# Self-attention in a decoder-and-fusion kernel: which key slot is reused first, and which score blocks come first

## The chip, the cores and the metric

One core of one Trainium2 chip runs the whole program. The metric is device time in microseconds (us); the median of three runs is given. TensorE is called PE in the views, VectorE DVE, ScalarE ACT, GpSimd POOL, and SyncE SP; SP issues most of the DMAs, in the order of its queue.

## The reference

The input is x, 4 batches of 1024 tokens of 512 channels, and a short context. A decoder layer comes first (self-attention, cross-attention, feed-forward, each with a layer norm and a residual), then a fusion with a gate. Only self-attention is touched by the change. It has 16 heads of 32 channels and is causal:

```python
q = einsum('btc,hcd->bhtd', xn, Wq) + bq      # k and v likewise
scores = einsum('bhtd,bhsd->bhts', q, k) / scale
scores = where(tril, scores, -inf)
attn = softmax(scores, axis=-1)
out = einsum('bhts,bhsd->bhtd', attn, v)
```

## The kernel before

**Units.** Self-attention is done in 32 units. A unit is a batch b (4), a group g of four heads (4), and a half h of the queries (2). With few exceptions h = 0 holds query tiles 0, 1, 6, 7 of 128 tokens and h = 1 holds tiles 2, 3, 4, 5, so that both have the same amount of causal work; in the first group of the first batch they are 0 to 3 and 4 to 7. The keys of a group stand in two halves, m = 0 (tokens 0 to 511) and m = 1 (512 to 1023). Both units of a group use the same two halves, except the very first unit, which needs m = 0 alone.

**Stacks.** Queries and keys are projected, split in a high and a low part, and stored to DRAM (L623, tensors `qd` and `kd`). `load_stacks` (L648) brings them back as stacks in SBUF: four key slots (`ks0` to `ks3`), one per key half, and three query slots (`qs0` to `qs2`), one per unit. `pile` (L641) loads one stack with three DMAs of 256 KB on SP's queue (L646). A list `order` keeps the key slots by age: a half that is not there yet goes into the oldest slot that none of the units in work needs, and each slot that a unit uses goes to the young end, in the order in which the loop (L652) meets the halves. The stacks of unit u + 2 are asked for when unit u begins.

**Two passes over the scores.** The first pass, `maxima` (L672), computes scores of a unit with queries on the rows, one PSUM bank of 512 columns at a time (L692, tiles `s`, four banks, shared with the projections), and VectorE takes the row minimum of each block (the scores are negated): with `tensor_reduce` (L702) where no mask is needed, with a masked custom operation (L699) and a read of its result on the diagonal. `put_maxima` (L716) combines them, transposes them on PE (`tpm`, L726), splits them in two rows (`mT`, L728 and L729) and sends them by ScalarE's DMA queue into two more rows of the query stack (L732). The second pass, `attend` (L735), computes the scores again with keys on the rows and with the maxima already subtracted (L755, tiles `st`, 98 rows instead of 96), takes the exponential on ScalarE (L760), masks the diagonal on POOL (L768), multiplies by the values (L785, `av`) and adds up the denominators, mostly on POOL (L809). For h = 1 it goes through the key tiles in the order 0, 5, 1, 4, 2, 3, so that the half m = 1 is done with before m = 0 is.

**A unit's score blocks.** There are 18 banks in a unit. A bank is a full block of 512 columns, or a pair of smaller ones: 128 and 384 columns of one head, or 256 and 256 of two heads. `maxima` writes them out head by head (L707 to L713): first the pair 128 and 384, then from every second head the pair 256 and 256, then the full blocks.

**What sets the order.** `run` (L115) merges three streams by the columns of work that they have done: the `attend` steps of unit u, the score steps still open of unit u + 1 with the first eight steps of unit u + 2 (L947 to L952; the first step only makes tiles, so seven banks), and projections of later groups (L854 to L871). Each engine then works in a fixed order, which the program's scheduler settles at build time from its own estimates, with priorities by stream.

Of the kernel before, what the change touches and what calls it, by code (L numbers as in the profile page):

```python
# [18 lines left out]
P = 128  # L19
# [10 lines left out]
HG = P // DH  # L30
# [22 lines left out]
def decoder_then_fusion(ctx: ExitStack, tc: tile.TileContext, x, ctxT, cols, rows,  # L53
# [399 lines left out]
    def self_attention(ph):  # L453
# [183 lines left out]
        def keys_of(u):  # L637
            b, g, _, tiles = units[u]
            return [(b, g, m) for m in range(tiles[-1] // NJ + 1)]

        def pile(stack, src, parts):  # L641

            for i, k in enumerate(parts):
                nc.sync.dma_start(raw(stack)[i * DH : (i + 1) * DH], src[k].rearrange("(r d) t -> d r t", d=DH))  # L646

        def load_stacks(u, since):  # L648

            b, g, h, _ = units[u]  # L650
            used = {k for w in range(since, u + 1) for k in keys_of(w)}
            for m, key in enumerate(keys_of(u)):  # L652
                if key in k_held:
                    slot = k_held.index(key)
                else:
                    slot = next(i for i in order if k_held[i] not in used)
                    k_held[slot] = key
                    pile(k_stacks[slot], k_dram[b, m, g], (0, 0, 1))
                order.remove(slot)
                order.append(slot)  # L660
                k_at[u, m] = k_stacks[slot]
            if (b, g) not in v_at:
                v_at[b, g] = vp.tile([P, NT, P], F32, tag="v", name=f"v_{b}_{g}")
            new = [key[2] for key in keys_of(u) if key not in v_held]
            v_held.update(keys_of(u))
            if new:
                kbs = slice(new[0] * NJ, (new[-1] + 1) * NJ)
                nc.sync.dma_start(v_at[b, g][:, kbs], v_dram[b,][:, kbs, g * P : (g + 1) * P])
            q_at[u] = q_stacks[u % len(q_stacks)]
            pile(q_at[u], q_dram[b, h, g], (0, 1, 0))  # L670

        def maxima(u):  # L672

            tiles = units[u][3]
            held = {}

            def begin():

                held["top"] = small.tile([P, HG, NJ, NG], F32, tag="top", name=f"top_{u}", bufs=2)
                held["least"] = small.tile([P, HG, NJ], F32, tag="least", name=f"least_{u}", bufs=2)  # L680

            def width(tile, m):
                return min(TG, (tile + 1) * P - m * TG)

            def scores(blocks):

                sc = ps_s.tile([P, TG], F32, tag="s", name="s_%d_%d_%d_%d" % (u, *blocks[0]))
                parts, at = [], 0
                for r, j, m in blocks:
                    part = sc[:, at : at + width(tiles[j], m)]  # L690
                    at += width(tiles[j], m)
                    nc.tensor.matmul(part, q_at[u][:KS, r, j * P : (j + 1) * P],  # L692
                                     k_at[u, m][:KS, r, : part.shape[-1]], start=True, stop=True)
                    parts.append(part)
                for part, (r, j, m) in zip(parts, blocks):
                    far = tiles[j] >= NJ
                    dst = held["top"][:, r, j, m : m + 1] if far else held["least"][:, r, j : j + 1]
                    if m == tiles[j] // NJ:
                        nc.vector.tensor_tensor_reduce(part, part, mask[:, TG - part.shape[-1] :],  # L699
                                                       1.0, TOP, ALU.add, ALU.min, dst)  # L700
                    else:
                        nc.vector.tensor_reduce(dst, part, AX.X, ALU.min)  # L702

            steps = [(0, begin)]
            at_width = {width(t, t // NJ): (j, t // NJ) for j, t in enumerate(tiles)}
            full = [(j, m) for j, t in enumerate(tiles) for m in range(t // NJ + 1) if width(t, m) == TG]
            for r in range(HG):  # L707

                banks = [[(r, *at_width[P]), (r, *at_width[3 * P])]] + [[(r, *at)] for at in full]
                if r % 2:  # L710
                    banks.insert(1, [(r - 1, *at_width[2 * P]), (r, *at_width[2 * P])])
                steps += [(sum(width(tiles[j], m) for _, j, m in blocks), lambda blocks=blocks: scores(blocks))
                          for blocks in banks]  # L713
            return steps + [(0, lambda: put_maxima(u, held["top"], held["least"]))]

        def put_maxima(u, top, least):  # L716

            tiles, qs = units[u][3], q_at[u]  # L720
            far = [j for j, tile in enumerate(tiles) if tile >= NJ]
            if far:
                nc.vector.tensor_reduce(least[:, :, far[0] :], top[:, :, far[0] :], AX.X, ALU.min)
            rows = HG * NJ
            tp = ps_of[Z["tpm"]][0].tile([rows, P], F32, tag=ps_of[Z["tpm"]][1], name=f"tpm_{u}")
            nc.tensor.transpose(tp, least.rearrange("p r j -> p (r j)"), ident)  # L726
            mT = [small.tile([rows, P], FR, tag=f"mT{k}", name=f"mT{k}_{u}", bufs=1) for k in range(2)]
            nc.vector.tensor_scalar(mT[0], tp, -1.0, None, ALU.mult)  # L728
            nc.vector.scalar_tensor_tensor(mT[1], tp, -1.0, mT[0], ALU.mult, ALU.subtract)  # L729

            for k in range(2):
                nc.scalar.dma_start(raw(qs[KS + k : KS + k + 1].rearrange("p r (j q) -> p (r j) q", q=P)),  # L732
                                    raw(mT[k]))
# [139 lines left out]
        def loads(u, since):  # L873
            return [(0, lambda: load_stacks(u, since))]

        run(pieces[0])
        early_banks[:] = Z["eb1"]
        load_stacks(0, 0)
        run(maxima(0), pieces[1] + loads(1, 0), speed=(Z["sp0"], 1))
        k = int(len(pieces[AHEAD]) * Z["p4f"])  # L880
        pieces[AHEAD + 1] = pieces[AHEAD][k:] + pieces[AHEAD + 1]
# [57 lines left out]
        for u in range(len(units)):  # L939
            if u and u + 2 < len(units):  # L940
                load_stacks(u + 2, u)
            main, tail = attend(u, tail)
            n = u % 2
            ahead, begun = begun, []
            if not ahead and u + 1 < len(units):
                ahead = maxima(u + 1)
            if u and u + 2 < len(units) and Z["phi%d" % n]:  # L947
                begun = maxima(u + 2)
                k = Z["phi%d" % n]
                first = begun[: k]  # L950
                first.insert(Z["tpl"], ahead.pop())
                ahead, begun = ahead + first, begun[k:]  # L952
            if u == first_late:
                fronts_of.close()
                rest = late_steps()
                total = sum(t for t, _ in rest)
            if u >= first_late:
                fill, part = [], Z["late"][u - first_late] * total
                while rest and (part > 0 or u + 1 == len(units)):
                    part -= rest[0][0]  # L960
                    fill.append(rest.pop(0))
            else:
                fill = pieces[u + AHEAD]
            run(main, ahead, fill, speed=(Z["main"], (Z["ahead%d" % n] if u < Z["alf"] else Z["ahead_l"]) if u else Z["a0"], Z["fill"]), sooner=(Z["so0"], Z["so1"], Z["so2"]))
# [842 lines left out]
```

## Time and profile before

| | us |
|---|---|
| median of 3 runs | 2146.06 |
| lowest, highest | 2144.63, 2152.42 |
| the profiled execution's own time | 2153.24 |
| its span, first to last instruction | 2151.5 |
| PE busy (of the span) | 2064.3 (96%) |
| DVE busy | 1452.1 (67%) |
| POOL busy | 1210.7 (56%) |
| ACT busy | 967.5 (45%) |

The profiled execution is 7.2 us over the median of the timed runs and near their highest. Self-attention takes the first 930 us or so: the last `st` product starts at 930.3 us. Engines' busy times overlap; the one that is busy nearly throughout is the one to look at first. Idle time of an engine is listed with what ended it, and of the other engines it costs nothing in itself. The granted clock of PE is given with the windows; 1.00 is full speed.

### The profile page before, as it was taken

To read this page: it belongs to the slowest core of one execution; us is meant where nothing else is said; L and a number is where in the kernel's file an instruction comes from. 1 tells how busy PE (TensorE), PEld (TensorE's weight loads), DVE (VectorE), ACT (ScalarE), POOL (GpSimd) and SP (SyncE) were. 2 spreads that over 40 slices of the span, in tenths; PEclk is the share of its full clock that TensorE was granted. 3 is DMA by queue.
4 is the path that set the end of the run, shared out by engine and by line. 5 is a ranking of instruction groups with operands and counts; after the bars stand their busy time and mean duration, and the time that the engine had idled before them with its cause. 6 is when DMAs were issued, how large, how long until landed. Compare 5 with 4: busy or idle time off the path is not lost.

```text
span 2151.5 us, 34750 instructions
## 1 busy us (share of the span) xinstructions
PE 2064.3 (96%) x11544; PEld 1568.7 (73%) x11544; DVE 1452.1 (67%) x3134; ACT 967.5 (45%) x2180; POOL 1210.7 (56%) x1257
## 2 busy tenths in 40 slices
PE   6999998999999989989999999999999999999997
PEld 5766676667667756457888887788788888888885
DVE  6587757665755587567676776877667846865667
ACT  3365555555565545435555557433322422232222
POOL 3288878888788877774555543512343524433323
PEclk9999999999999998999999999999999999999998
DMA  8866767677666567662323122965576457655631
GB/s 245 258 186 168 218 203 216 182 243 219 190 174 186 158 171 213 206 204 79 99 84 103 50 79 86 332 210 170 182 238 198 166 175 237 207 175 171 220 113 39
DMA packets 241321, 379.36 MB, mean 176 GB/s; under 512 B 35948, under 2 KB 104284, under 8 KB 239094
## 3 DMA queue, kind: packets, MB, share of 16 engines
q1 hardware_dynamic: 215532, 348.32, 52.4%
q10 hardware_dynamic: 25610, 28.83, 4.4%
q8 instruction: 92, 1.51, 0.3%
q14 instruction: 87, 0.71, 0.1%
HBM read 251.71 MB, written 124.81 MB: 175 GB/s over the span
## 4 chain that ended last, share of the span: by engine, by line
PE 76%; DMA 7%; DVE 7%; POOL 4%; issue 2%; ACT 1%; SPq 1%; ACTq 0%; DVEq 0%; POOLq 0%
PE acc L1495 15%; PE ph L1473 14%; PE st L755 5%; PE s L692 5%; PE av L785 5%; PE po_c L102 4%; PE pq_x L102 3%; PE pk L102 3%; PE pv L102 3%; PE pg_o L102 3%; PE po_x L102 3%; PE pq L102 3%; POOL pT L809 2%; PE sc_c L87 2%; PE av_c L1139 1%
## 5 line engine op out<-in xcount | busy, mean ns | idle before, releaser
L809 POOL TENSOR_TENSOR pT<-pT,pT 128x256 f32<-128x256 f32 (+3 forms) x369 | 551.6, 1514 | 106.0 <-PE av L785 97.1
L760 ACT ACTIVATE pT<-st 128x512 f32<-128x512 f32 (+2 forms) x640 | 322.3, 559 | 171.2 <-PE st L755 122.9
L1495 PE MATMUL acc<-wf,hs 128*128 128x512 f32 x1536 | 392.1, 393 | 0.9 <-DVE y L1507 0.9
L1495 PEld LDWEIGHTS acc<-wf,hs 128*128 128x128 f32 x1536 | 285.8, 188 | 63.1 <-ACT inT L74 1.3
L699 DVE CUSTOM_DVE_ANT_0 s<-s,mask 128x128 f32<-128x128 f32 (+3 forms) x512 | 244.5, 504 | 99.6 <-PE s L692 97.1
L692 PE MATMUL s<-ks,qs 96*128 96x512 f32 (+3 forms) x768 | 230.2, 371 | 23.0 <-DMA qs<-qd 7.3
L702 DVE TENSOR_REDUCE top<-s 128x1 f32<-128x512 f32 x256 | 171.9, 684 | 104.4 <-PE s L692 103.9
L755 PE MATMUL st<-qs,ks 98*128 98x256 f32 (+2 forms) x888 | 227.8, 340 | 4.7 <-ACT pT L760 2.0
L1473 PE MATMUL ph<-inT,wp 128*128 128x512 f32 x768 | 205.3, 396 | 3.1 <-DVE p L1431 1.2
L755 PEld LDWEIGHTS st<-qs,ks 98*128 98x128 f32 x888 | 149.4, 192 | 63.7 <-issue 20.2
L692 PEld LDWEIGHTS s<-ks,qs 96*128 96x128 f32 x768 | 135.6, 194 | 81.0 <-issue 17.0
L1473 PEld LDWEIGHTS ph<-inT,wp 128*128 128x128 f32 x768 | 143.9, 189 | 36.6 <-DVE gp_o L1568 1.8
L785 PE MATMUL av<-pT,v 128*32 128x512 f32 (+3 forms) x1776 | 155.1, 454 | 4.1 <-POOL pT L768 4.1
L1473 PE MATMUL ph<-inX,wp 128*128 128x512 f32 x576 | 151.4, 395 | 1.1 <-DVE inX L75 1.1
L768 POOL TENSOR_SCALAR_AFFINE_SELECT pT<-pT 128x256 f32<-128x256 f32 x256 | 103.7, 421 | 73.6 <-ACT pT L760 73.1
L1473 PEld LDWEIGHTS ph<-inX,wp 128*128 128x128 f32 x576 | 108.4, 189 | 25.2 <-issue 1.3
L1542 POOL TENSOR_TENSOR y<-y,row_bf 128x512 f32<-128x512 f32 x32 | 41.6, 1304 | 132.6 <-DMA y<-x 72.1
L1481 ACT ACTIVATE hs<-ph 128x512 fp32r<-128x512 f32 x64 | 38.3, 599 | 172.2 <-DVE ph L1431 99.4
L102 PE MATMUL pk<-xn_s,wk 128*128 128x512 f32 x384 | 106.1, 412 | 4.9 <-DVE top L702 3.0
L102 PE MATMUL pv<-wv,xn_s 128*128 128x256 f32 x768 | 108.1, 286 | 2.5 <-DVE least L699 1.6
L102 PEld LDWEIGHTS pv<-wv,xn_s 128*128 128x128 f32 x768 | 102.1, 192 | 11.4 <-DVE top L699 2.9
L1118 POOL TENSOR_TENSOR p_c<-p_c,inv_c 128x512 f32<-128x512 f32 x64 | 68.4, 1069 | 73.9 <-DVE inv_c L1117 58.6
(262 smaller groups left out, 3907.8 us busy)
## 6 DMA issues: line engine op xcount, KB each, us to landing
wp<-wpd SPq DMA_DIRECT2D x168, 256.0 KB
ks<-kd SPq DMA_DIRECT2D x96, 256.0 KB
qs<-qd SPq DMA_DIRECT2D x96, 256.0 KB
wf<-w2fd SPq DMA_DIRECT2D x48, 512.0 KB
kd<-k SPq DMA_DIRECT2D x64, 256.0 KB
qd<-q SPq DMA_DIRECT2D x120, 128.0 KB
wpd<-wp SPq DMA_DIRECT2D x56, 256.0 KB
x<-in_x SPq DMA_DIRECT2D x32, 256.0 KB
```

The source lines that it names most:

```text
L102: nc.tensor.matmul(held["ps"], a_at(a()[i], c), b_at(b()[j], c), start=not bias and c == 0 and k == 0, stop=c == NC - 1 and k == 2)
L692: nc.tensor.matmul(part, q_at[u][:KS, r, j * P : (j + 1) * P], k_at[u, m][:KS, r, : part.shape[-1]], start=True, stop=True)
L699: nc.vector.tensor_tensor_reduce(part, part, mask[:, TG - part.shape[-1] :], 1.0, TOP, ALU.add, ALU.min, dst)
L702: nc.vector.tensor_reduce(dst, part, AX.X, ALU.min)
L755: nc.tensor.matmul(st[:, i], k_at[u, kb // NJ][:KM, r + i, (kb % NJ) * P : (kb % NJ + 1) * P], q_at[u][:KM, r + i, c0:], start=True, stop= ...
L760: nc.scalar.activation(held[kb][(r + i) // 2][:, at : at + k, c0:], st[:, i : i + k], AF.Exp, scale=-QSCALE)
L768: nc.gpsimd.affine_select(out=t, in_=t, compare_op=ALU.is_ge, fill=0.0, base=0, pattern=[[0, 2], [1, P]], channel_multiplier=-1)
L785: return nc.tensor.matmul(held["av"][r * DH : (r + 1) * DH, c0:], v_at[b, g][:, kb, r * DH : (r + 1) * DH], held[kb][r // 2][:, r % 2, c0: ...
L809: eng.tensor_tensor(t[:, :, c0:], t[:, :, c0:], p[:, :, c0:], ALU.add)
L1118: nc.gpsimd.tensor_tensor(pr, pr, inv.unsqueeze(2).to_broadcast([P, HH, S]), ALU.mult)
L1473: nc.tensor.matmul(ps, w[:, q, c], x[:, r, c], start=c == 0 and m == 0, stop=c == HC - 1 and m == 2)
L1495: mm = nc.tensor.matmul(accs[j], hidden[b, n, f][:, q, j * P : (j + 1) * P], w2s[b, f][:, r], start=begins and m == 0, stop=ends and m == 2)
```

## The change

Two things are changed. In `load_stacks` the halves of a unit with h = 1 are gone through backwards, so that the slot of m = 1 becomes the older of the two in the list. In `maxima` all banks of a unit are listed and then sorted by the highest key half that they need; the full blocks come first among those of one half, then the pairs of 256, then the pairs of 128 and 384.

```diff
@@ load_stacks
-            for m, key in enumerate(keys_of(u)):
+            for m, key in list(enumerate(keys_of(u)))[:: -1 if h else 1]:
@@ maxima
-            for r in range(HG):
-
-                banks = [[(r, *at_width[P]), (r, *at_width[3 * P])]] + [[(r, *at)] for at in full]
-                if r % 2:
-                    banks.insert(1, [(r - 1, *at_width[2 * P]), (r, *at_width[2 * P])])
-                steps += [(sum(width(tiles[j], m) for _, j, m in blocks), lambda blocks=blocks: scores(blocks))
-                          for blocks in banks]
+            banks = [[(r, *at)] for r in range(HG) for at in full]
+            banks += [[(r, *at_width[2 * P]), (r + 1, *at_width[2 * P])] for r in range(0, HG, 2)]
+            banks += [[(r, *at_width[P]), (r, *at_width[3 * P])] for r in range(HG)]
+            banks.sort(key=lambda blocks: max(m for _, _, m in blocks))
+            steps += [(sum(width(tiles[j], m) for _, j, m in blocks), lambda blocks=blocks: scores(blocks))
+                      for blocks in banks]
```

## The prediction

> **What bounds the kernel now.** I read the page's busy times, then the waits of PE, then time by 10 us windows with the granted clock, then the places where PE waits for a stack.
>
> ```profile
> PE 2064.3 (96%) x11544; PEld 1568.7 (73%) x11544; DVE 1452.1 (67%) x3134; ACT 967.5 (45%) x2180; POOL 1210.7 (56%) x1257
> ...
> PE 76%; DMA 7%; DVE 7%; POOL 4%; issue 2%; ACT 1%; SPq 1%; ACTq 0%; DVEq 0%; POOLq 0%
> ```
>
> PE is the bound. The change gives it the same products, so it can only touch PE's idle time (2151.5 - 2064.3 = 87 us in the whole span), and what the clock loses behind an idle stretch. The waits of PE that a score block has for a stack are these:
>
> ```profile
> PE s L692 <- DMA qs<-qd: 7.3, 3, 3.1
> PE s L692 <- DVE top L702: 4.5, 4, 1.8
> ...
> PE s L692 <- DMA kd<-k: 2.5, 2, 2.3
> ...
> PE st L755 <- DMA qs<-mT: 1.8, 2, 1.4
> ```
>
> The columns are total, times and longest. The first and third lines are what the change aims at: 9.8 us. Gone through by place: 1.94 us at 37.2 (unit 0), 3.13 at 56.3 (unit 1), 2.28 at 344.5 (unit 12), 0.21 at 405.2 (unit 14), 2.23 at 553.7 (unit 20). The two named after the store kd are bursts in which that store was issued right behind the load of the query stack; the scores don't read it, so I take them for the same wait. All other units find their stacks in time. The last of these waits is the pattern:
>
> ```profile
> 538.44 3.65 SPq L623 DMA_DIRECT2D qd<-q  x4
> 544.60 1.27 SPq L646 DMA_DIRECT2D ks<-kd  x3
> 545.91 1.38 SPq L646 DMA_DIRECT2D qs<-qd  x3
> ```
> ```profile
> 551.00 0.50 PE L692 MATMUL s<-ks,qs 96*128 96x512 f32 x1
> 553.73 0.87 PE L692 MATMUL s<-ks,qs 96*128 96x128 f32 x2 [2.23 <-DMA qs<-qd]
> 554.40 5.32 PE L102 MATMUL pq<-xn_s,wq 128*128 128x512 f32 x12
> ```
> ```profile
> 553.00:554.00 1.00, 0.27 (x2) 0.30 (x2) 0.00 (x0) 0.00 (x0) 0.37 (x1) 0.63 1.02 383
> 554.00:555.00 1.00, 1.00 (x4) 0.90 (x4) 0.36 (x3) 0.00 (x0) 0.00 (x0) 0.50 1.11 348
> ...
> 559.00:560.00 1.00, 1.00 (x4) 0.71 (x3) 0.00 (x0) 0.19 (x1) 0.00 (x0) 0.50 0.00 0
> ```
>
> First SP's queue: the late key half, then the query stack right behind it. Then PE: the first score block of unit 20 waits 2.23 us, and the wait ends with the query stack. Then windows of 1 us (third number from the end is the clock): half speed until 560, 3.4 us lost over the 10 us window (its mean clock is 0.66). So this stall costs 2.2 + 3.4 = 5.6 us. The one at 344.5 costs 2.3 + 1.7 = 4.0 us (clock 0.83 in 340 to 350).
>
> [...]
>
> **Step 1, the slots.** Before, m = 0 of a new group gets the slot of the old m = 0, which is the last to come free, since `attend` ends on tiles of that half. The order of the built program shows SP issuing m = 1 first, some rows of stores later m = 0, then the query stack. After the change m = 0 takes the early slot and is issued first, m = 1 is issued late, and in every pair of units the query stack is still issued behind the late key half. The number of loads and their bytes are the same.
>
> **Step 2, the score order.** Before, the first bank of an h = 0 unit (128 and 384 columns) needs both halves. After, seven to twelve banks need m = 0 alone. But each needs the query stack, and that lands last in the row above. A score that no longer waits for the late half waits for the query stack behind it. So the direct gain is between 0 and 0.21 + 4.0 + 5.6 = 9.8 us; I take 0, since the row names the query stack as the end of the wait.
>
> [...]
>
> **Step 3, what the scheduler moves.** In the built order, before unit 20, the last two `st` products on the old m = 0 stack of unit 17 stand behind a group of 12 key products (541.30 to 544.04 in the trace, 2.74 us); after, they stand in front of it. The late slot then comes free up to 2.7 us earlier. The query stack can't use all of that: its stores are issued until 538.44 + 3.65 = 542.09, and the smallest distance from a store to its reload that I find is 2.2 us (a key store out at 43.43, its reload at 45.59), so about 544.3 instead of 545.91: 1.6 us. DMA is busy for 0.88 of the time from 540 to 550, so I credit half: 0.8 us of idle time and half of the clock's loss, 1.7 us. Together -2.5 us, with ends 0 and -5.6. For unit 12 no such group moves, and SP stands in front of POOL's split of a weight (L270, 334.0 to 335.3) in both orders, with one more key load (0.42 us of issue) behind that split: 0, ends -4.0 and +0.4.
>
> At the start two stores of values (L594) now stand on SP ahead of the third key load and the three query loads of unit 1. They wait for ACT's copies at 48.24 and after; before, the query loads were out by 48.69. With DMA full (1.04 of its time at 50 to 56) the two stores of 128 KB put 256 KB ahead, at 210 to 317 GB/s about 1 us. PE has waited 3.13 us there and its clock is at half already, so 1 us more is 1 us: +1, ends 0 and +4 (all of the delay of issue, 2.6 us, and some clock).
>
> **Step 4, VectorE.** Nothing is added; what is moved is its load. Durations by shape between 100 and 850 us: reduce 512 is 685 ns; masked 512, 384, 256, 128 are 702, 569, 443, 300, each with a read of 139 or 140.
>
> ```profile
> L702 DVE TENSOR_REDUCE top<-s 128x1 f32<-128x512 f32 x232 | 156.0, 685 | 95.7 <-PE s L692 95.2
> L699 DVE CUSTOM_DVE_ANT_0 s<-s,mask 128x512 f32<-128x512 f32 x116 | 81.5, 702 | 35.8 <-PE s L692 35.5
> L699 DVE CUSTOM_DVE_ANT_0 s<-s,mask 128x384 f32<-128x384 f32 x116 | 66.1, 569 | 1.2
> ```
>
> A bank costs 0.69 us if it is a plain block, 0.84 masked, 1.15 as 128 and 384, 1.17 as 256 and 256. The first seven banks of an h = 0 unit were 2 x 1.15 + 1.17 + 3 x 0.69 + 0.84 = 6.4 us and become 7 x 0.69 = 4.8. So 1.6 us move from there to the eleven that are left for the next unit (h = 1: 6.5 to 5.3, 1.2 us). A unit lasts (930 - 62) / 32 = 27 us, and VectorE is busy about 0.65 of it, so some 9 us stand open. I cost this at 0. Behind these reads stand the four score banks, which projections use too, and `mT`; the open time hides them. If the cover is gone, the price is 1.6 us in each place where VectorE is full. Windows of 10 us with VectorE at 9.5 or more are seven between 100 and 900, such as:
>
> ```profile
> 110.00:120.00 10.00, 9.82 (x65) 6.38 (x58) 9.90 (x23) 4.70 (x9) 9.03 (x7) 1.00 0.73 242
> 430.00:440.00 10.00, 9.91 (x74) 6.99 (x73) 9.95 (x30) 6.30 (x13) 9.76 (x12) 1.00 0.84 267
> ```
>
> (after the length come PE, weight loads, DVE). So its ends are 0 and 7 x 1.6 = +11 us. PE is near full in both windows, so there even a full VectorE held it up little.
>
> **The sum.** 0 - 2.5 + 0 + 1 + 0 = -1.5 us: 2153.24 becomes 2151.7 for a profiled execution. That execution is 7.2 us over the median. The terms are stalls of the program's order, not of that execution alone, so I take them off the median: 2146.06 - 1.5 = 2144.5.
>
> **The rivals.**
>
> *The wait goes altogether.* The first scores need less, the query stack comes in time with the earlier release, and the stalls at units 12, 14 and 20 vanish with their slow stretches: -9.8 us. The same reshuffle may take away the 1.79 us wait for VectorE at 375.5 with its slow stretch (clock 0.79 and 0.87 in 370 to 390, 3.4 us). 2146 - 9.8 = 2136, with the second 2131. For it: the late slot comes free earlier or as early before most units. Against: the query stack is last on SP in all of them. 16%.
>
> *VectorE becomes the late one.* The costly pairs now stand together at the end of a unit's scores, just ahead of `tpm`; where VectorE is full, PE waits for a bank, and `mT` comes late for `st`. It decides once a unit's scores are issued faster than about 0.9 us a bank (15.8 us of VectorE work for 18). Price +11, and +1 from the start: 2158. For it: waits of PE for `top` and `least` are there now (4.5 and 1.2 us for `s`). Against: 35% open time. 16%.
>
> *It does nothing.* The named change happens, the query stack hides it, and the scheduler's moves cancel: 2146, next to my forecast and in one case with it. In such a reshuffle one stall with a slow stretch may appear or go, 4.0 to 5.6 us either way, so forecast and this together span 2138 to 2152. 68%.
>
> **How the numbers follow.** Faster or slower by over 0.5% means beyond 10.7 us (about what a measurement of this kernel can tell from no change): below 2135.3 or above 2156.8. Of the first rival's 16% some three quarters pass that bound, with 3% from two more slow stretches gone: 15% faster. Of the second, likewise three quarters and 3%: 15% slower. The rest, 70%, is within. The range takes in the first rival with its second part, 2131, and the second, 2158, and leaves out what lies beyond these, under 2 in 10.
>
> **What would show it.** The wait at unit 20 (first scores after its query load) shorter than 2.2 us, with less half clock behind it: step 3 right. Score waits on stacks gone at unit 12 too: step 2 wrong, the first rival. SP issuing the query stack ahead of the late key half: step 1 read wrongly. PE's waits for `top`, `least` and `mT`, projections' included, are 4.5 + 3.0 + 1.6 + 1.4 + 1.2 + 1.1 + 3.7 = 16.5 us now; over 22: step 4 wrong. The wait at 56.3 us longer than 3.1: the start as said. A changed length of the parts after 950 us would be outside all of this and would make the prediction wrong for no reason given here.

## The result and the profile after

The changed kernel takes 2159.06 us (median of 10 runs, 2153.80 to 2161.93). The kernel before, timed beside it, takes 2151.32 us (10 runs, 2144.63 to 2158.06). The ratio is 1.0030, with a 95% interval of 1.0017 to 1.0044: 4 to 9 us slower. The time lies 1 us above the predicted range, and 14.6 us above the forecast. These divide into 5.3 us by which the median of three runs had been low (2151.32 - 2146.06), 7.7 us of the change, and the 1.6 us that the forecast took off.

The profiled execution of the changed kernel is the shortest of its ten (2153.80, span 2152.0), so its page looks almost like that of before, whose profiled execution (2153.24) was 1.9 us over the median of ten. First its busy times and its chain by engine; in the change's file L692 to L702 stand two lines lower, all that follows three.

```profile
PE 2065.9 (96%) x11544; PEld 1567.7 (73%) x11544; DVE 1459.6 (68%) x3134; ACT 968.2 (45%) x2180; POOL 1207.8 (56%) x1257
...
PE 78%; DMA 7%; DVE 7%; POOL 4%; issue 2%; ACT 1%; SPq 1%; DVEq 0%; POOLq 0%; ACTq 0%
```

PE has the same work and nearly the same idle time (86.1 us, 87.2 before). Its waits (total, times, longest):

```profile
PE s L694 <- DMA qs<-qd: 8.7, 4, 3.1
...
PE pvc L102 <- DVE wvc L75: 5.1, 1, 5.1
PE s L694 <- DVE least L701: 4.5, 5, 1.8
PE pv L102 <- DVE least L701: 3.5, 3, 1.7
```

The stack waits that the change aims at are still there: 8.7 us, where 9.8 were. One wait for VectorE's split of a late weight, `wvc`, has grown from 0.8 to 5.1 us.

**What the profile can't show, the clocks of all runs do.** Each timed run lists its span and its mean granted clock. I call (1 - clock) x span the loss at half clock, and the span less this loss the rest. (The clock is listed to three digits, which is 1 us either way in a single run; half-clock time in which PE idles counts as loss too.) Means over all runs of the two kernels in the experiments below, those of the result included for the change (errors are of the mean):

| | runs | span | loss at half clock | rest |
|---|---|---|---|---|
| before | 122 | 2150.7 | 32.4 (0.4) | 2118.3 (0.2) |
| the change | 17 | 2156.6 | 38.6 (1.1) | 2118.0 (0.7) |

The span grew by 5.9 us, the loss at half clock by 6.2, the rest not at all, to within 0.7. So the change doesn't make PE wait longer or work more. It makes PE run longer at half speed. Everything below is about why.

### The profile page after: what moved, and what is told of

The parts are those of the page before. It is cut to its first block, busy times and chain, and to the rows that moved or that the text cites. A ratio compares the mean times of both kernels' runs of the same rounds, so it can differ in the third digit from the quotient of the medians.

```text
span 2152.0 us, 34713 instructions
## 1 busy us (share of the span) xinstructions
PE 2065.9 (96%) x11544; PEld 1567.7 (73%) x11544; DVE 1459.6 (68%) x3134; ACT 968.2 (45%) x2180; POOL 1207.8 (56%) x1257
## 4 chain that ended last, share of the span: by engine, by line
PE 78%; DMA 7%; DVE 7%; POOL 4%; issue 2%; ACT 1%; SPq 1%; DVEq 0%; POOLq 0%; ACTq 0%
PE acc L1498 15%; PE ph L1476 14%; PE st L758 5%; PE av L788 5%; PE s L694 5%; PE po_c L102 4%; PE pq_x L102 3%; PE pv L102 3%; PE pk L102 3%; PE pg_o L102 3%; PE po_x L102 3%; PE pq L102 3%; POOL pT L812 3%; PE sc_c L87 2%; DMA qs<-qd 2%
## 5 line engine op out<-in xcount | busy, mean ns | idle before, releaser
L701 DVE CUSTOM_DVE_ANT_0 s<-s,mask 128x512 f32<-128x512 f32 (+3 forms) x512 | 240.9, 512 | 97.1 <-PE s L694 94.8
```

## How the half-speed stretches come about

Windows of 0.02 us around each step of the clock give the stretches to the point. Behind 100 us and up to 940 they are, before: 345.0-348.5, 375.8-382.6, 553.3-560.1, 792.2-799.0, 833.1-850.2; in the change: 341.4-344.8, 372.1-379.0, 433.6-437.0, 570.1-573.5, 788.6-798.8, 822.7-826.1, 839.8-846.6, 867.1-873.9. Each is 3.41 us long or a multiple, and all begin and end on one grid: in every one of the 20 profiles of this study the records of the clock fit one period of 3.4133 us to within 0.001 us. Where the grid begins differs by execution (the span starts 0.30 us off the grid before, 2.49 us in its repeat). I call one period a cell.

I cut each profile into the cells of its own grid, from 25 to 995 us, and took PE's idle time in a cell and the clock of the next:

```
cell at full clock, idle under 0.8 us       4822 cells    1 followed by half clock
                    0.8 to 1.6 us            229 cells   69
                    over 1.6 us              190 cells  181
cell at half clock, idle under 0.2 us        262 cells   24 stay at half
                    0.2 to 0.4 us             19 cells   11
                    over 0.4 us              139 cells  134
```

So in these profiles it isn't the length of one wait that counts but the sum of idle time in a cell: behind over 1.6 us idle, about half a cell, the next one ran at half clock in 181 of 190 cases, which loses 1.7 us. The full-clock cells that a wait of 1.6 us or longer touches tell the two apart: half clock follows none of the 28 that have under 0.8 us idle, 13 of the 59 with 0.8 to 1.6, and 162 of the 170 with more. Why some cells in the middle group are followed and others aren't, these rows don't show.

This bears on what the credit of unit 20 was worth. In the trace of PE in the changed kernel, the wait of unit 20 is the first line, and two waits behind it are the others:

```profile
553.50 0.47 PE L694 MATMUL s<-ks,qs 96*128 96x512 f32 x1 [1.50 <-DMA qs<-qd]
...
568.22 0.50 PE L758 MATMUL st<-qs,ks 98*128 98x256 f32 x2 [1.11 <-ACT pT L763]
569.39 4.60 PE L102 MATMUL pk<-xn_s,wk 128*128 128x512 f32 x12 [0.67 <-DVE xn_s L75]
```

Windows cut on the grid (after the length: PE, weight loads, VectorE, ScalarE, GpSimd, granted clock, DMA share, GB/s):

```profile
566.69:570.10 3.41, 1.63 (x8) 1.04 (x7) 2.74 (x6) 3.41 (x8) 3.41 (x4) 1.00 0.91 304
570.10:573.52 3.42, 3.42 (x10) 2.65 (x9) 2.92 (x8) 0.50 (x2) 3.18 (x6) 0.50 0.29 92
```

The wait of unit 20 fell from 2.23 to 1.50 us, and no half-speed stretch follows it here. But that is where the border of the cells fell in this execution: 1.05 us of the wait lie in one cell and 0.46 in the next. In the repeat of the changed kernel (e3; the runs with an e stand in the next section) the wait is 1.65 us and lies whole in one cell, and half speed follows:

```profile
555.17 0.75 PE L694 MATMUL s<-ks,qs 96*128 96x512 f32 x1 [1.65 <-DMA qs<-qd]
```
```profile
551.77:555.19 3.42, 1.77 (x15) 1.41 (x11) 2.97 (x16) 1.79 (x4) 3.42 (x6) 1.00 1.05 251
555.19:558.60 3.41, 3.41 (x8) 2.74 (x9) 1.25 (x4) 0.00 (x0) 0.03 (x1) 0.50 0.92 277
```

The repeat of the kernel before (e4) waits 2.20 us there and has one cell at half speed behind it, as many as e3. And e14, which comes from the kernel before, waits 2.08 us for unit 20; a border cuts the wait, PE is idle for 1.24 and 1.21 us in the two cells, and the clock stays up:

```profile
560.20 0.52 PE L692 MATMUL s<-ks,qs 96*128 96x128 f32 x2 [2.08 <-DMA qs<-qd]
```
```profile
555.58:558.99 3.41, 2.18 (x15) 0.87 (x13) 3.41 (x13) 1.98 (x5) 3.41 (x7) 1.00 1.05 219
558.99:562.41 3.42, 2.21 (x11) 1.91 (x12) 1.07 (x6) 0.00 (x0) 0.99 (x1) 1.00 1.09 335
562.41:565.82 3.41, 3.41 (x28) 1.66 (x30) 2.07 (x5) 1.27 (x2) 0.00 (x0) 1.00 0.37 121
```

Behind unit 20, 1.11 and 0.67 us now stand in one cell: PE is idle for 1.78 of 3.41 us, and the next cell runs at half speed. e3 has the same two waits and the same cell at half speed, from 572.3 us. Before, one wait of 1.22 us stood there alone, cut by a border, and nothing followed:

```profile
570.87 3.02 PE L102 MATMUL pk<-xn_s,wk 128*128 128x512 f32 x12 [1.22 <-DVE top L702]
```

That cell and one other place are what both profiles of the change have and none of the four with the earlier order of scores (before, e4, e1, e13) has: the other is 6.8 us at half speed from 867 and 869 us, behind the grown wait for `wvc`. Together these are 10.2 us at half speed, or 5.1 us of loss, near the 6.2 of the table. But other reshuffles below lose as much elsewhere, and e10, with the change's order on PE, has no half speed at 570 and no smaller loss.

## The experiments

All times are beside runs of the kernel before on the same chip (its median was 2150.5 to 2156.9 there). "Places" are those of PE's 10,248 products, in the built order of the whole program, at which a product of another tile stands than in the kernel before (the 24 products that e17 and e18 add are left out of the count). Loss and rest are differences of means to the kernel before beside it; their errors are 1.1 to 2.6 us and 0.8 to 2.0 us.

| kernel | places | median us | ratio, 95% interval | loss | rest |
|---|---|---|---|---|---|
| e4 before again | 0 | 2150.94 | 0.9999 [0.9988, 1.0009] | +0.5 | -1.0 |
| e1 slots only | 94 | 2150.66 | 0.9995 [0.9983, 1.0008] | +1.2 | -2.3 |
| e13 before, query first | 0 | 2151.53 | 1.0007 [0.9989, 1.0025] | +0.3 | +1.1 |
| e3 change again | 2709 | 2158.84 | 1.0037 [1.0025, 1.0050] | +8.0 | -0.9 |
| e2 order only | 2713 | 2164.42 | 1.0058 [1.0041, 1.0075] | +9.4 | +3.8 |
| e5 sorted to unit 27 | 3929 | 2162.66 | 1.0027 [1.0011, 1.0042] | +7.1 | -1.6 |
| e6 sorted from unit 28 | 470 | 2169.93 | 1.0067 [1.0048, 1.0085] | +8.3 | +4.7 |
| e7 no low split | 2795 | 2162.40 | 1.0031 [1.0016, 1.0047] | +8.8 | -3.0 |
| e8 heads in half | 2627 | 2167.64 | 1.0055 [1.0035, 1.0076] | +6.1 | +5.0 |
| e9 pairs last | 2354 | 2163.64 | 1.0062 [1.0049, 1.0075] | +8.4 | +5.3 |
| e10 change, query first | 2709 | 2156.20 | 1.0023 [1.0012, 1.0035] | +8.6 | -3.7 |
| e14 nudge before | 1237 | 2159.12 | 1.0040 [1.0025, 1.0055] | +5.4 | +3.1 |
| e15 nudge after | 2757 | 2162.01 | 1.0038 [1.0017, 1.0059] | +6.4 | +2.9 |
| e16 sooner, before | 1042 | 2171.96 | 1.0091 [1.0066, 1.0115] | +12.8 | +7.1 |
| e17 fill, before | 296 | 2155.84 | 1.0021 [1.0004, 1.0037] | +2.9 | +1.9 |
| e18 fill, change | 2729 | 2163.09 | 1.0049 [1.0030, 1.0068] | +9.5 | +0.8 |
| e11 half reads, before | 3614 | 2209.03 | 1.0269 [1.0254, 1.0284] | +37.1 | +21.1 |
| e12 half reads, change | 3986 | 2233.26 | 1.0377 [1.0359, 1.0394] | +50.3 | +31.3 |

(e15 and e18 move 1,182 and 91 places against the change.)

### Which edit: e1 to e4

e1 takes the first edit alone, e2 the second; e3 and e4 repeat both kernels.

```diff
 e1: load_stacks as changed, maxima as before
 e2: maxima as changed,
-            for m, key in list(enumerate(keys_of(u)))[:: -1 if h else 1]:
+            for m, key in enumerate(keys_of(u)):
```

> The kernel before with the first edit alone (halves gone through backwards for h = 1). PE's built order then differs from before in 94 of 10,248 places. Theory A (the score order costs the time, by the order it gives PE and VectorE): as before, within 0.1%, 2149 to 2153 us. Theory B (the swapped slots cost it, as the half that is stored last is now loaded last): as slow as the whole change, about 2158 us. Theory C (the difference is a draw of executions): within 0.15% of before, like all four kernels of this set.

> The changed kernel with the first edit undone, so the sorted banks alone. PE's built order differs from the whole change in 114 places. Theory A: as slow as the whole change, 0.2 to 0.4% over before, 2156 to 2160 us. Theory B: as before. If the sorted order helps only with the swapped slots, it is slower than the whole change, as the half that its first banks need is then the late one: by up to the 10 us of stack waits, 2168 us.

> The changed kernel once more, for a second profile and to see whether the 0.3% stands on another set of executions. Theories A and B: ratio 1.002 to 1.004. Theory C: 0.999 to 1.0015.

> The kernel before, as a kernel of its own, for a second profile and for how far equal kernels lie apart: ratio 0.9985 to 1.0015 by all theories; a ratio outside tells that differences of 0.3% can't be told from none.

The slots alone do nothing that can be measured, the score order alone costs 12 us, both repeats hold: theory A stands, B and C fall. e2's time lies above the 2156 to 2160 of theory A, on the way to the 2168 that I had put for a sorted order whose first half comes late. With the sorted order the slots are worth some 5.6 us (2164.42 - 2158.84), though the two kernels also differ in 114 places on PE; with the earlier order nothing can be measured.

### Which place: e5 to e8

```diff
 e5: the sorted banks for u < 28 only;  e6: for u >= 28 only (e5, e6: slots as changed)
 e7, in split():
+        if uid.startswith("wvc_"):
+            nc.vector.memset(raw(lo), 0.0)
+            return
 e8:
-            banks.sort(key=lambda blocks: max(m for _, _, m in blocks))
+            banks.sort(key=lambda blocks: (max(m for _, _, m in blocks), blocks[0][0]))
```

> The changed kernel with the earlier order of scores put back for the last four units (28 to 31); units 0 to 27 keep the sorted order. Theory L (late): most of the loss lies between 780 and 960 us, where VectorE's splits of the late weights and GpSimd's long additions meet, and there about 5.4 of the 6 us of PE idle and lost clock stood. L expects 2151 to 2154 us. Rival E (everywhere): the bunched costly pairs cost a little in all units; 28 of 32 units would keep 7/8 of the loss of 7.7 us: 2156 to 2160.

> The reverse: the earlier order of scores in units 0 to 27, the sorted order in 28 to 31 alone, slots as in the change. L expects nearly the whole loss, 2156 to 2160; E expects an eighth of it, 2151 to 2153. If both halves come out between, the loss belongs to no place, and the moved schedule behind each edit is the cause.

> The changed kernel, in which the four low parts of the late weights wvc are filled with zeros by VectorE, which reads nothing, where they were the difference of two SBUF tiles (the kernel leaves out that product term's value; PE still runs it). Theory L in its narrow form (the two-input subtractions are held up to 4 us each beside GpSimd's additions, PE waits 5 us for them and then runs at half clock): the wait of pvc for wvc falls from 5 to under 1 us, and the time to 2152 to 2155. If the place is right but the subtractions are not what is late, the wait stays for another operand, and the time stays at 2157 to 2161.

> The changed kernel with its banks sorted by half and then by head: still all banks of the first half first, but plain and masked banks alternate within a half, so that the costly masked pairs no longer stand side by side. Bunching (step 4 of the prediction: VectorE's reads pile up behind the masked pairs) expects the loss gone, 2150 to 2154. If it is the order by halves, or the place of the late work, 2156 to 2161.

I had a place (780 to 960 us) and a culprit: the 5.1 us wait for wvc, which shows in the changed kernel, in e3, e6, e8 and e10 (5.1, 4.6, 7.4, 4.3, 4.5 us). It fell. e5 has no such wait in its list and is still slower, e6 is the slowest of the set, and the halves add up to more than the whole. All four came out above every range that I had put; the kernel before takes 2156.91 us on this chip, 5 to 6 us more than on the others, and the ranges didn't reckon with it. e7 removes the wait, and its rest is 3.0 us under that of before (error 1.2), but its loss is 8.8 us above, and its time is no better than the change's. PE's waits in e7 where that wait had been:

```profile
880.79 0.50 PE L697 MATMUL s<-ks,qs 96*128 96x512 f32 x1 [1.10 <-DVE top L707]
883.02 1.46 PE L697 MATMUL s<-ks,qs 96*128 96x512 f32 x3 [1.09 <-DVE side_vc L347]
```

Two waits of 1.1 us within one cell, and the clock is at half from 882.9 to 893.2. e8 takes the bunching of masked pairs away and isn't faster than the change (1.0055, where e3 has 1.0037): bunching isn't the price either, as far as a kernel can tell that moves 1,873 places against the change.

### Sorted banks, or any other order: e9, e14, e15, e16

```diff
 e9, head by head, on the kernel before:
-                banks = [[(r, *at_width[P]), (r, *at_width[3 * P])]] + [[(r, *at)] for at in full]
+                banks = [[(r, *at)] for at in full]
                 if r % 2:
-                    banks.insert(1, [(r - 1, *at_width[2 * P]), (r, *at_width[2 * P])])
+                    banks.append([(r - 1, *at_width[2 * P]), (r, *at_width[2 * P])])
+                banks.append([(r, *at_width[P]), (r, *at_width[3 * P])])
 e14 (on before), e15 (on the change): 'ahead0' and 'ahead1', 1.5 -> 1.45
 e16 (on before): 'so1', 20 -> 30
```

> The kernel before with one neutral shuffle: still head by head, halves mixed as ever, but in each head the plain blocks come first and the masked pairs last. Theory S (sorting by halves is what costs): 2151 to 2153 on a chip where the kernel before takes 2151.5, within 0.15% of it. Rival N (the built order around before's banks leaves fewer half-speed stretches of TensorE than others do, and any shuffle loses them): slower by 4 to 14 us, with PE's idle time up to 980 us as before (50 to 57 us) and its loss at half clock above 29 us, where the three runs with the earlier order have 22 to 27.

> The kernel before with its banks untouched and one weight of the interleaving nudged (the scores ahead at 1.45 of the main stream's speed, where it is 1.5), which moves 1,237 of PE's 10,248 places, half as many as the change. Theory N (the order built around the earlier banks leaves fewer half-speed stretches than its neighbours, and any move of it loses them) expects 4 to 14 us slower, the idle time of PE about as before and the loss at half clock above 29 us. Theory S (only another order of the banks costs) expects within 3 us of the kernel before.

> The changed kernel with the same nudge (1,182 places move). If the sorted order as such carries the cost, this stays 5 to 10 us above the kernel before. If the cost belongs to one built order, it may land anywhere from 0 to 16 us above the kernel before, with no bound to the change's 7.

> The kernel before, banks untouched, with another weight moved (the scores' head start in priority 30 where it is 20), which moves 1,042 of PE's places. N expects 4 to 14 us slower again; S expects within 3 us of the kernel before.

This is the answer to what the sorting costs: nothing of its own that these runs can tell. A shuffle inside each head, with the halves mixed as ever, costs 12 us; two nudges that leave the banks alone cost 9 and 22. All 13 measured kernels in which 296 places or more differ from before (the change among them, e11 and e12 left aside) are slower, by 0.21 to 0.91%; the three with none or 94 aren't. They aren't 13 independent draws: nine have the sorted banks in some or all units, and e17 has added products, so that e9, e14 and e16 are the only plain reshuffles of the kernel before. In each of the 13 the loss at half clock is larger, by 2.9 to 12.8 us, whether the rest fell or rose (in six it rose by 3 to 7 us, so there waits cost too). Theory N stands, theory S falls. My expectation for e16, 4 to 14 us, was too low. e15 stands 11.6 us above before, over the 5 to 10 of a sorting that costs as such and inside the 0 to 16 of one built order. And the profile of e14 again is the shortest of its twelve runs (2153.67, median 2159.12): by it alone the nudge would look free, and its loss up to 980 us is 25.6 us, not above 29 as N expected. Over all its runs the loss is 5.4 us above before.

### The query stack's place: e10, e13

```diff
             used = {k for w in range(since, u + 1) for k in keys_of(w)}
+            q_at[u] = q_stacks[u % len(q_stacks)]
+            pile(q_at[u], q_dram[b, h, g], (0, 1, 0))
...
-            q_at[u] = q_stacks[u % len(q_stacks)]
-            pile(q_at[u], q_dram[b, h, g], (0, 1, 0))
```

> The changed kernel with the query stack loaded ahead of the key halves; PE's order stays exactly that of the change. Step 2 of the prediction says that the sorted order gains nothing at the stacks because the query stack is issued last and lands last. If so, with the query stack first, the 8.7 us of PE's waits for query stacks fall below 4, and the late key half, needed only after six banks, causes none: 3 to 9 us faster than the change, 2150 to 2156 where the kernel before takes 2151.5. If the landing is set by the queue's total bytes and not by the order, the waits move to the key half or stay, and the time stays within 2 us of the change (2157 to 2161).

> The kernel before with the query stack loaded ahead of the key halves; PE's built order is that of the kernel before in every place. With it, slots and score order make a table of two by two: query first alone, sorted alone, both, neither. Step 2 read in full: in the earlier order the first bank needs both key halves and the query stack, so the wait only changes its name, from the query stack to the late key half, and the time stays within 2 us of the kernel before. If the query stack's own issue place is what is late, 3 to 6 us faster.

e10 changes no place in PE's order of the change, only SP's queue. Of its PE waits on DMA for score blocks these are left:

```profile
PE s L694 <- DMA x<-in_x: 2.2, 1, 2.2
PE s L694 <- DMA qs<-qd: 2.1, 1, 2.1
```

8.7 us became 4.3: the waits of units 12 and 20 (2.12 and 1.50 us in the change) are gone, unit 1 waits 2.1 us where it waited 3.1, and the first line is the wait of unit 0 at 37 us under another name (1.9 in the change). The rest is 3.7 us below that of before (error 1.4): the query stack's late place was what kept the sorted order from its gain in waiting. But the loss at half clock stands 8.6 us above before, so the kernel stays 3 to 8 us above before, and its ratio of 1.0023 isn't clearly below the change's 1.0030 and 1.0037. e13, the same under the earlier order, does nothing, as step 2 says. Its waits for score blocks are 10.0 us (9.8 before); unit 20 still waits 2.3 us, now for the key half. No kernel here is measurably faster than the one before.

### VectorE with room: e11, e12

```diff
+                    reach_to = TG - part.shape[-1]
+                    part = part[:, : max(part.shape[-1] // 2, P)]
```

> The kernel before, in which VectorE reads only the first half of the columns of each score block wider than 128 (the maxima are taken over part of the keys), so that its reads take about half of their 190 us or so. Control for the next run. If VectorE's lateness carries much of PE's idle time, this is 5 to 20 us faster than the kernel before; the built order changes in a third of PE's places too.

> The changed kernel with the same halved reads. If the sorted order costs time by making VectorE late (step 4 of the prediction, or its late splits), VectorE now has room, and this stands within 2 us of the kernel before with halved reads. If the cost has nothing to do with VectorE's load (where idle time of any cause falls on the clock's steps), the difference of 6 to 8 us between the two orders stays, or takes any sign between -8 and +14.

Both expectations failed by far. With shorter reads the scheduler puts score blocks earlier, ahead of their stacks; a row of e11's waits:

```profile
PE s L692 <- DMA qs<-qd: 46.0, 15, 6.0
```

46 us where 7.3 were. So these two tell nothing of VectorE, but they show what it costs when score blocks are put ahead of their stacks: in e11 21 us more rest and 37 us more half clock.

### A wait filled with idle work: e17, e18

```diff
                 sc = ps_s.tile([P, TG], F32, tag="s", name="s_%d_%d_%d_%d" % (u, *blocks[0]))
+                if u in (20,) and "warm" not in held:
+                    held["warm"] = True
+                    for _ in range(24):
+                        nc.tensor.matmul(sc[:, :P], ident_r, ident_r, start=True, stop=True)
```

> The kernel before with 24 products of 128 columns that nobody reads, put on PE just ahead of unit 20's first bank, into that bank, so that PE works for most of the 2.2 us in which it waited for the query stack. In all four profiles with the earlier order that keep the wait at 2.2 us (before, its repeat, e6 and e13) half-clock cells follow it. If the clock falls by the idle time in a cell of 3.41 us (none of 2,470 full-clock cells with under 0.8 us idle was followed by a half-clock one, to within one), the wait shows under 1 us, the stack lands when it did, and no half-clock cell lies between 550 and 562 us. If the clock falls for the stall whatever PE does, the cells stay. In time the fill is worth 1.7 to 3.4 us at most; 296 of PE's places move as well, which by theory N may cost 0 to 8 us: 2147 to 2159 where the kernel before takes 2150.5.

> The changed kernel with the same fill; only 91 of PE's places move. The wait of unit 20 (1.50 to 1.65 us) disappears and no half-clock cell follows before 562 us; the cell at 570 us, where two waits of 1.1 and 0.6 us stand close together, is untouched by the fill. Time within 4 us of the change (2154 to 2162).

The fill stands where the wait was. PE in e17, and its cells on the grid of that execution:

```profile
559.74 0.50 PE L696 MATMUL s<-ks,qs 96*128 96x512 f32 x1
560.08 2.46 PE L691 MATMUL s<-ident_r 128*128 128x128 f32 x21
```
```profile
558.58:561.99 3.41, 3.03 (x28) 2.36 (x28) 2.76 (x9) 1.09 (x3) 3.41 (x6) 1.00 1.03 224
561.99:565.41 3.42, 3.42 (x21) 2.97 (x21) 1.62 (x4) 0.00 (x0) 0.14 (x1) 1.00 1.01 320
```

The transfers run as before (DMA 1.0), there is no wait of 2.2 us, and the clock stays at 1.00. Ten other profiles (e11 and e12 aside) have a wait of 2 us or more for unit 20; half-clock cells follow it in nine, and the tenth is e14, where a border cuts it. Without the fill the first cell above would have held about 2.3 us of idle time (an estimate: the 1.9 us of fill in it and the 0.38 that are idle). So here it was PE's own idle time that made the clock fall, and 1.9 us of work that nobody needs kept it at 1.00. In e18 no half-clock cell lies between 550 and 575 us. Neither kernel is faster for it: e18's 2163.09 us lies 1 us above what I expected, and the time of e17 can't be told from a small loss by its moved places. Where it went, the next cells of e17's profile show:

```profile
575.65:579.06 3.41, 2.36 (x19) 1.21 (x11) 1.97 (x4) 3.41 (x8) 3.33 (x3) 1.00 0.90 323
579.06:582.47 3.41, 2.71 (x19) 1.16 (x19) 3.05 (x6) 1.54 (x4) 3.25 (x7) 0.50 0.82 235
582.47:585.89 3.42, 3.42 (x11) 2.74 (x9) 1.68 (x6) 0.60 (x1) 3.09 (x5) 0.50 0.68 138
```

Some 20 us on, two waits of 0.5 us and smaller ones add up to 1.05 us in a cell, the clock falls, and behind that half-clock cell, with 0.71 us idle, stands another.

## Why the prediction was wrong, step by step

- **What bounds the kernel: right.** From the last denominator product to the end the profiles have 1208.7 and 1207.7 us before (the repeat second), 1207.6 and 1208.7 in the change; it starts at 942.8 and 941.4 us before, at 944.4 and 947.3 in the change. So the change lies ahead of it, in self-attention.
- **Step 1, slots: right.** SP in the changed kernel, ahead of unit 20, still issues the late key half and then the query stack:

```profile
539.56 3.49 SPq L623 DMA_DIRECT2D qd<-q  x4
544.21 1.28 SPq L646 DMA_DIRECT2D ks<-kd  x3
545.54 1.38 SPq L646 DMA_DIRECT2D qs<-qd  x3
```

- **Step 2, no direct gain: right, and tested** by e10 and e13.
- **Step 3, the scheduler's moves: right for unit 20's wait, wrong in the clock.** Unit 20's wait fell by 0.73 us, and by 0.55 in the repeats (0.8 credited). The 1.7 us of clock credited with it aren't shown: half speed is gone behind it in one profile, where a border cuts the wait, and in the repeats one cell follows it before and after the change alike. Unit 12's wait is 2.12 us (2.28 before; 0 credited). The start was not later: 3.12 us, 3.13 before, where I had put +1. Left out was what the moved work meets next: 1.7 us were lost at 570.1.
- **Step 4, VectorE's bunching: costed at 0, and that held.** PE's waits for `top`, `least` and `mT`, the smallest included, are 13.9 us (17.5 before; 16.6 and 18.4 in the repeats), far from my 22. e8 points the same way. The rival "VectorE becomes the late one" gave 2158 and thus nearly the time, by luck and not for its reason.
- **The step that failed** is in "it does nothing": "in such a reshuffle one stall with a slow stretch may appear or go, 4.0 to 5.6 us either way". The terms of waiting were about right (-0.8 + 1 = +0.2 forecast; the rest moved by -0.3 +- 0.7). The clock's term was -1.7 and came out at +6.2, or 3.6 cells at 1.7 us. "Either way" was wrong: 13 of 13 reshuffles lost, the three plain ones 9 to 22 us. I priced slow stretches one by one behind single stalls, and didn't see that short waits add up in a cell.
- **The base.** "The terms are stalls of the program's order, so I take them off the median" took 2146.06 of three runs; the later sets of the same kernel have medians of 2150 to 2157. That alone is 5.3 us of the miss.

Open is why the earlier order loses so little. That it does is shown (32.4 us, where the reshuffled kernels lose 35 to 45); which of its waits stand so well apart, and whether by the order's making or by luck, no run here decides.

## What to carry to other kernels

With PE as the bound, look at its idle time per 3.41 us, not at the longest wait: two waits of 1.1 and 0.7 us in one cell were followed by a cell at half clock here, as the one wait of 1.65 us in e3 was, and a wait that was taken away was made up for elsewhere here (e7, e17). Separate each timed run into clock loss and rest before reading a profile: one profile, here by chance the shortest of ten, can hide the whole effect. And measure a neutral reshuffle beside a meant one: where a scheduler sets the order, moving 296 places or more had a price of 4 to 22 us here, and a gain must be larger than that.

## What was not expected of the hardware

The grid of the clock (3.4133 us in all 20 profiles) is the main thing, told above. The other is the wait for wvc. VectorE's rows in the changed kernel:

```profile
860.72 7.96 DVE L75 TENSOR_TENSOR wvc<-chunk,wvc 128x512 fp32r<-128x512 f32 x2 [0.50 <-ACT wvc L74]
...
869.69 0.66 DVE L75 TENSOR_TENSOR wvc<-chunk,wvc 128x512 fp32r<-128x512 f32 x1
```

and GpSimd's at that time:

```profile
861.28 5.89 POOL L812 TENSOR_TENSOR pT<-pT,pT 128x512 f32<-128x512 f32 x3
```

In the changed kernel the same subtraction takes 0.66 us alone and 7.96 us for two beside GpSimd's additions; before, the four took 0.67 to 1.37 us each. That the additions hold it up, as my expectation for e7 took it, isn't shown: no run here moved them away, and before, two of the four took 1.27 us together beside additions of GpSimd:

```profile
866.71 1.27 DVE L75 TENSOR_TENSOR wvc<-chunk,wvc 128x512 fp32r<-128x512 f32 x2
```
```profile
864.62 5.63 POOL L809 TENSOR_TENSOR pT<-pT,pT 128x512 f32<-128x512 f32 x2
```
